# Finishing the message stage's last chunk of nodes in spans of 4, 2 and 1 blocks, with the last block added in the next pass

## The chip, the cores and the metric

The kernel runs on one core of a Trainium2 chip. The metric is the time of one execution in microseconds of device time; the times given are medians of several executions. One further execution was recorded by the hardware profiler, and all profile lines come from it. TensorE is called PE here, VectorE DVE, ScalarE ACT, GpSimd POOL and SyncE SP; PEld are PE's weight loads.

## The reference

A small graph network over N = 6250 nodes with 64 features and E = 206250 directed edges. Every stage normalises each node's row, applies relu, and adds what comes back along the edges. What matters here are the last two stages:

```python
# stage 3: a message for each edge, summed by its end, then a root
x_ = relu(relu(E @ w1 + b1) @ w2 + b2)
msg = sigmoid(x_ @ Bw + Bb) * Vp[src] + (x_ @ Cw + Cb)
M = clip(msg, EPS) ** 2
mean = segment_sum(M, dst) / max(count, 1)
x = x + sqrt(mean)
# stage 4: three rounds of propagation over the same graph
h = maximum(layernorm(x), 0)
embs = acc = h
for _ in range(3):
    embs = segment_sum(norm[:, None] * embs[row], col)
    acc = acc + embs
x = x + acc / 4
```

## The kernel before, in words

**Layout.** The nodes stand in 49 blocks (NB) of 128 rows, seven blocks (CB) to a chunk, seven chunks (NC). The graph is held in DRAM as a dense matrix of edge counts in fp8, `A[c]` for the columns of chunk c. A piece `A[c][:, blocks(k), :]` has 128 x 7 x 896 counts, 784 KB. A sum over neighbours is a matrix product of such pieces with node values; the values are split into three bf16 parts (`split`, L712), which stand in the tile `U3`.

**The message loop** (`slot`, L1599, called from L1645). The edges are sorted by their end and worked on in G = 202 groups of 1024. Slot i does one step of each of several groups: it turns the edge features of group i (L1527), runs the two layers for groups i-1 and i-2 (L1531), the gates and shifts for group i-3 (L1541, L1545), multiplies and clips group i-4 (L1555 to L1557; L1555 reads the rows of `Vp` that POOL has fetched by eight indirect DMAs, L1519, into one of four buffers), squares and splits it, sums group i-5 over its edges (L1578) and adds group i-6 to its nodes in `H` (L1583 ff). PE, DVE and ACT run in the order in which the code is written (`manual_schedule`, L1644).

**What is done beside it.** `todo` is a list of pieces of extra work, and each slot takes n of them (L1616), so many that the list is empty when the next chunk of nodes is finished; half is done ahead of the squares and half at the slot's end. There are three kinds. A *crossing* (L1420) turns up to four 128 x 128 squares of a piece with PE (L1425) and compares them with the mirrored piece by DVE (L1431): the kernel checks that the matrix is symmetric. There are 28 pairs of chunks, each with 14 crossings. A *partial sum* (L1438) multiplies one half (448 columns) of a piece with the values of the seven blocks of chunk i, 21 matmuls of 64 output rows (L750), and DVE adds the result to `Y` (L1450). `here` and `there` load the pieces, through SP's queue. Crossings, partial sums and the squares of the messages share two PSUM buffers, `p_sum`.

**The order of the work.** When the messages of chunk c are complete, `finished(c)` (L1485) divides and takes the root, adds to `X`, normalises and splits the result into `U3`: 14 passes of DVE and four of ACT, one after another. Then `plan` puts the pieces of chunk c into `todo`: the four pairs of `CROSS[c]` and 14 partial sums. So chunks 0 to 5 of the first round's matrix product are summed in the loop. The pairs of `FIRST` fill the slots before chunk 0 is finished. Chunks 0 to 5 are finished at the ends of slots 35, 64, 93, 122, 151 and 180, chunk 6 at the end of slot 207, the last.

**Behind the loop.** For the first round of propagation, only chunk 6's part is left: for every half s, 21 matmuls (L1700 to L1707), the addition to `Y` (L1708), and for every second half seven matmuls with `twice`, which turn `Y` back to nodes (L741), and `propagated` (L1676), which scales and splits the result for the next round. The second and the third round are `gather` (L1180): for every chunk, 49 blocks times seven, one matmul of 192 columns each (L1190), from pieces loaded six ahead.

Of the kernel before, what the change touches and what calls it, by code (L numbers as in the profile page):

```python
# [16 lines left out]
P = 128  # L17
# [600 lines left out]
def fast(ctx, tc, bad, x, src, dst, edge_attr, W3, b3, W4, b4, w1, b1, w2, b2, Bw, Bb, Cw, Cb,  # L618
# [52 lines left out]
    missed = const.tile([P, 3], F32, name="missed")  # L671

    def blocks(c):
        return slice(c * CB, (c + 1) * CB)

    def over_features(v, n=CB):
        return v.unsqueeze(2).to_broadcast([P, n, D])
# [14 lines left out]

    def normed(h, X_c):

        m = stat.tile([P, CB], F32, name="m")
        nc.vector.tensor_reduce(m, X_c, axis=AX.X, op=OP.add)
        nc.vector.tensor_scalar_mul(m, m, 1.0 / D)
        nc.vector.tensor_sub(h, X_c, over_features(m))
        q = stat.tile([P, CB, D], F32, name="q")
        nc.vector.tensor_mul(q, h, h)  # L700
        v = stat.tile([P, CB], F32, name="v")
        nc.vector.tensor_reduce(v, q, axis=AX.X, op=OP.add)
        nc.scalar.activation(v, v, AF.Sqrt, bias=eps, scale=1.0 / D)
        nc.vector.reciprocal(v, v)
        nc.vector.scalar_tensor_tensor(h, h, 0.0, over_features(v), op0=OP.max, op1=OP.mult)

    def of_nodes(pool):

# [1 line left out]

    def split(u, U3, c):
        u3 = U3[:, blocks(c), :, :]  # L712
        nc.scalar.activation(u3[:, :, 0, :], u, AF.Copy)
        r = stat.tile([P, CB, D], F32, name="r")
        nc.vector.tensor_sub(r, u, u3[:, :, 0, :])
        nc.scalar.activation(u3[:, :, 1, :], r, AF.Copy)
        nc.vector.tensor_sub(u3[:, :, 2, :], r, u3[:, :, 1, :])
# [455 lines left out]

    def normed_and_split(h, U3, c, scale):
        normed(h, X[:, blocks(c), :])
        u = stat.tile([P, CB, D], F32, name="u")
        nc.vector.tensor_mul(u, h, over_features(scale[:, blocks(c)]))
        split(u, U3, c)

    def gather(apool, wpool, psum, U3, then, beside=iter(())):  # L1180


        for c in range(NC):
            p = [psum.tile([P, 512], F32, name=f"p_acc{q}") for q in range(4)]
            for k in range(NC):
                t = apool.tile([P, CB, W], COUNT, name="piece")
                nc.sync.dma_start(t, A[c][:, blocks(k), :])
                for d in range(CB):
                    for b in range(CB):
                        nc.tensor.matmul(  # L1190
                            p[d // 2][:, d % 2 * 3 * D:(d % 2 + 1) * 3 * D],
                            t[:, b, d * P:(d + 1) * P],
                            U3[:, k * CB + b, :, :].rearrange("p t f -> p (t f)"),
                            start=(k == 0 and b == 0 and d % 2 == 0),
                            stop=(k == NC - 1 and b == CB - 1 and d in (1, 3, 5, 6)))
                for _ in range(2 - (c > 0 or k > 4)):
                    next(beside, None)
            z = wpool.tile([P, CB, D], F32, name="zg")
            for q in range(4):
                n = min(2, CB - 2 * q)  # L1200
                nc.vector.tensor_reduce(  # L1201
                    z[:, 2 * q:2 * q + n, :],
                    p[q][:, :n * 3 * D].rearrange("p (d t f) -> p d f t", t=3, f=D),
                    axis=AX.X, op=OP.add)
            then(c, z)
# [173 lines left out]
    with ExitStack() as ph:  # L1379
# [9 lines left out]


        CROSS = (((0, 6), (0, 1), (0, 2), (0, 0)), ((1, 6), (1, 2), (1, 3), (1, 1)),
                 ((2, 6), (2, 3), (2, 4), (2, 2)), ((3, 6), (3, 4), (3, 5), (3, 0)),
                 ((4, 6), (4, 5), (4, 0), (4, 1)), ((5, 6), (5, 0), (5, 1), (5, 2)))
        FIRST = ((3, 3), (4, 4), (5, 5), (6, 6))
        unlike = cpool.tile([P, 28 * 2 * CB], F32, name="unlike")

        def order(pairs):
            ks = [k for _, k in pairs]
            return [(pairs[0][0], k)
                    for k in ks + [k for k in range(NC) if (pairs[-1][0], k) not in pairs]]  # L1400

        here_of = list(FIRST) + [at for pairs in CROSS for at in order(pairs)]
        there_of = list(FIRST) + [at for pairs in CROSS for at in pairs]
        held = {}

        def here(n):

            if n < len(here_of):
                i, k = here_of[n]
                t = held["here", i, k] = piece_pool.tile([P, CB, W], COUNT, name="piece")  # L1410
                nc.sync.dma_start(t, A[k][:, blocks(i), :])

        def there(n):

# [23 lines left out]
        def partial(i, s):  # L1438

            t = held["here", i, s // 2]  # L1440
            p = ps_a.tile([P, 512], F32, name="p_sum", bufs=2)
            for b in range(CB):
                spread(p, U3, i * CB + b, t[:, b, s % 2 * CW:(s % 2 + 1) * CW], CW,
                       i * CB, CB)

            def added():
                if i == 0:
# [5 lines left out]

        todo, crossings, asked = [], [], []

        def plan(pairs, sums):
            for at, (i, k) in enumerate(order(pairs) if sums else pairs):
                asked.append((i, k))
                todo.append((here, len(asked)))
                if at < len(pairs):  # L1460
# [21 lines left out]
                if then:  # L1482
                    read.append(then)

        def finished(c):  # L1485

            t = H[:, blocks(c), :]
            nc.vector.tensor_mul(t, t, over_features(n1[:, blocks(c)]))

            nc.vector.tensor_scalar_max(t, t, 1e-30)  # L1490
            nc.scalar.activation(t, t, AF.Sqrt)
            nc.vector.tensor_mul(t, t, over_features(some[:, blocks(c)]))
            nc.vector.tensor_add(X[:, blocks(c), :], X[:, blocks(c), :], t)
            normed_and_split(H[:, blocks(c), :], U3, c, norm3)
            if c < NC - 1:
                plan(CROSS[c], True)

        here(0)
        there(0)
        plan(FIRST, False)  # L1500
        last = {b: g for g in range(G) for b, _, _ in halves(g)}
        ends = [last[c * CB + CB - 1] for c in range(NC)]

        BC_AT, M_AT, SUM_AT, ADD_AT = 3, 4, 5, 6
        of = [{} for _ in range(G)]
        ends = [e + ADD_AT for e in ends]

        def loaded(g):
            of[g]["e"] = mpool.tile([P, J * D], F32, name="e", bufs=6)
# [70 lines left out]
        def added_to_nodes(g):  # L1583
# [5 lines left out]
            for k, (b, q0, q1) in enumerate(halves(g)):  # L1589
# [4 lines left out]
                else:  # L1594
                    nc.vector.tensor_scalar(H[:, b, :], r, part, None, op0=OP.mult)
                    begun.add(b)
            return [b // CB for b, _, _ in halves(g) if last[b] == g and b % CB == CB - 1]

        def slot(i):  # L1599
            def at(later):  # L1600
# [12 lines left out]
            read_them()  # L1613
            if at(1):
                layer(i - 1, w1_d, "eT", "p_1")
            n = -(-len(todo) // max(min(k for k in ends if k >= i) + 1 - i, 1))  # L1616
            some_of(n - n // 2)
            if at(M_AT):
                squared(i - M_AT)
# [16 lines left out]
            some_of(n // 2)  # L1636
            if at(SUM_AT):
                summed(i - SUM_AT)
            for c in done:
                finished(c)  # L1640

        for g in range(4):
            loaded(g)
# [2 lines left out]
                slot(i)  # L1646
            read_them()

        assert not todo and len(crossings) == 28 * 2 * CB


        nc.vector.tensor_reduce(missed[:, 2:3], unlike, axis=AX.X, op=OP.add)
# [14 lines left out]
    with ExitStack() as ph:  # L1667
# [2 lines left out]
        psum = ph.enter_context(tc.tile_pool(name="ps4", bufs=1, space=PSUM, reuse_waits="tile"))  # L1670
        upool = ph.enter_context(tc.tile_pool(name="upool", bufs=1, reuse_waits="tile"))

        for layer in range(3):
            V3 = of_nodes((upool, node)[layer]) if layer < 2 else None

            def propagated(c, y):  # L1676
                z = wpool.tile([P, CB, D], F32, name="z")
                s3 = over_features(norm3[:, blocks(c)])
                nc.vector.tensor_mul(z, y, s3)
                if V3 is not None:  # L1680
                    u = wpool.tile([P, CB, D], F32, name="u")
                    nc.vector.tensor_mul(u, z, s3)
                    split(u, V3, c)
                h = H[:, blocks(c), :]
                nc.vector.tensor_add(h, h, z)
                if V3 is None:
                    o = X[:, blocks(c), :]
                    nc.vector.scalar_tensor_tensor(o, h, 0.25, o, op0=OP.mult, op1=OP.add)
                    lo, hi = c * W, min((c + 1) * W, N)
                    full = (hi - lo) // P  # L1690
                    nc.sync.dma_start(
                        out[lo:lo + full * P, :].rearrange("(b p) f -> p b f", p=P),
                        o[:, :full, :])
                    if lo + full * P < hi:
                        nc.sync.dma_start(out[lo + full * P:hi, :], o[:hi - lo - full * P, full, :])

            if layer:
                gather(apool, wpool, psum, U3, propagated)
            else:
                for s in range(CS):  # L1700
                    if s % 2 == 0:
                        whole = apool.tile([P, CB, W], COUNT, name="piece")
                        nc.sync.dma_start(whole, A[s // 2][:, blocks(NC - 1), :])
                    t = whole[:, :, s % 2 * CW:(s % 2 + 1) * CW]
                    p = psum.tile([P, 512], F32, name="p_sum", bufs=2)
                    for b in range(CB):
                        spread(p, U3, NB - CB + b, t[:, b, :], CW, NB - CB, CB)  # L1707
                    nc.vector.tensor_add(Y[:, s, :], Y[:, s, :], p[:, :CW])  # L1708
                    if s % 2:
                        propagated(s // 2, to_nodes(  # L1710
                            psum, Y[:, s - 1:s + 1, :].rearrange("p s w -> p (s w)"), CB))
            U3 = V3


def gnn_kernel(tc, *args):
# [38 lines left out]
```

## Time and profile before

| what | us |
|---|---|
| median of 3 runs (4157.1 to 4163.57) | 4158.35 |
| the profiled execution | 4192.68 |
| its span, first to last instruction | 4190.8 |
| message loop, first gather of rows to the last slot | about 1000 to 3730 |
| last chunk's finishing (DVE L1488 to L717, then one addition) | 3730.1 to 3740.3 |
| the rest of the first round | 3740 to 3785 |
| second round, first matmul at | 3785.2 |
| third round, to the end | 3983 to 4190.8 |

How the views read: the page gives busy shares in 40 slices of the span (here 104.8 us each), the granted clock of PE in tenths, and the groups of instructions by line. A timeline line has the start in us, the busy time in us, the engine, the source line, the operation, output<-inputs with the shape, the count, and in brackets the idle time of the engine just before and what ended it. A line of a table of stretches has the stretch, its length, the busy time of PE, PEld, DVE, ACT and POOL with the count of instructions, the granted clock of PE, the DMA share and GB/s. In the loop a slot can be told by the start of its L1555: slot i is the (i-3)rd of the 202.

### The profile page before, as it was taken

To read this page: it belongs to the slowest core of one execution; us is meant where nothing else is said; L and a number is where in the kernel's file an instruction comes from. 1 tells how busy PE (TensorE), PEld (TensorE's weight loads), DVE (VectorE), ACT (ScalarE), POOL (GpSimd) and SP (SyncE) were. 2 spreads that over 40 slices of the span, in tenths; PEclk is the share of its full clock that TensorE was granted. 3 is DMA by queue.
4 is the path that set the end of the run, shared out by engine and by line. 5 is a ranking of instruction groups with operands and counts; after the bars stand their busy time and mean duration, and the time that the engine had idled before them with its cause. 6 is when DMAs were issued, how large, how long until landed. Compare 5 with 4: busy or idle time off the path is not lost.

```text
span 4190.8 us, 60773 instructions
## 1 busy us (share of the span) xinstructions
PE 3129.4 (75%) x24366; PEld 2232.6 (53%) x24366; DVE 2074.5 (50%) x5097; ACT 1237.4 (30%) x2061; POOL 1609.1 (38%) x1894
## 2 busy tenths in 40 slices
PE   1799989996665666666676757766766777689999
PEld 1788889994333333333333333433333343349999
DVE  6999934322554544444545544544454454462111
ACT  3677710001333322332333323323332333220000
POOL 5000010002666655655555555556555655510000
PEclk9999999997777778877877777778777787789999
DMA  3243366653222222222222222222222222125665
GB/s 114 56 109 98 97 218 193 197 184 96 58 60 60 58 55 67 57 61 59 64 63 61 59 56 71 60 53 57 75 56 54 63 73 61 45 90 186 200 207 156
DMA packets 229379, 388.81 MB, mean 93 GB/s; under 512 B 93801, under 2 KB 139801, under 8 KB 228830
## 3 DMA queue, kind: packets, MB, share of 16 engines
q1 hardware_dynamic: 170478, 322.28, 24.7%
q0 software_dynamic: 55104, 60.65, 7.2%
q8 instruction: 193, 3.16, 0.3%
q10 hardware_dynamic: 3504, 1.90, 0.2%
q14 instruction: 100, 0.82, 0.1%
HBM read 340.48 MB, written 44.21 MB: 92 GB/s over the span
## 4 chain that ended last, share of the span: by engine, by line
PE 47%; DVE 22%; another core or an unknown queue 12%; issue 10%; ACT 7%; DMA 1%; POOL 0%; ACTq 0%; DVEq 0%; SPq 0%; POOLq 0%
PE p_acc L1190 18%; PE p_bc L1545 7%; PE p_sum L750 5%; PE p L1531 5%; DVE to L1570 3%; DVE hd L888 3%; ACT h L1535 2%; PE p_s L1578 2%; DVE lo L888 2%; DVE m L1555 2%; DVE m L1556 2%; DVE junk L1431 2%; PE p_bc L1541 2%; PE p_sum L1425 2%
## 5 line engine op out<-in xcount | busy, mean ns | idle before, releaser
L1519 POOL DMA_INDIRECT v<-Vp_dram,src_g x1616 | 1537.6, 952 | 1489.9 <-DVE m L1555 682.2
L1190 PE MATMUL p_acc<-U,piece 128*128 128x192 bf16 x9604 | 800.3, 246 | 11.9 <-DMA piece<-A 9.4
L1190 PEld LDWEIGHTS <-piece 128*128 128x128 fp8e4 x9604 | 795.4, 98 | 17.1 <-DMA piece<-A 9.6
L1545 PE MATMUL p_bc<-BC,h 128*128 128x256 f32 x1616 | 582.8, 489 | 33.7 <-issue 32.0
L1425 PE MATMUL p_sum<-ident_b,piece 128*128 128x128 bf16 x1372 | 167.4, 247 | 527.5 <-issue 190.9
L1425 PEld LDWEIGHTS <-piece 128*128 128x128 fp8e4 x1372 | 116.0, 111 | 693.2 <-issue 469.9
L1431 DVE SCALAR_TENSOR_TENSOR junk<-p_sum,there 128x512 bf16<-128x512 f32 (+1 forms) x392 | 242.4, 618 | 489.1 <-remote 329.9
L1545 PEld LDWEIGHTS p_bc<-BC,h 128*128 128x128 f32 x1616 | 339.4, 232 | 206.7 <-issue 170.7
L1555 DVE TENSOR_TENSOR m<-p_bc,v 128x512 f32<-128x512 f32 x202 | 139.7, 691 | 558.9 <-ACT p_bc L1550 444.5
L750 PE MATMUL p_sum<-piece,U 128*64 128x448 fp8e4 x2058 | 287.1, 391 | 109.2 <-issue 91.4
L1535 ACT ACTIVATE h<-p,b_c 128x512 f32<-128x512 f32 x404 | 263.5, 692 | 275.8 <-PE p_sum L1425 116.3
L1531 PE MATMUL p<-h,w_d 128*128 128x512 f32 x404 | 269.6, 748 | 87.7 <-ACT h L1535 58.8
L907 ACT ACTIVATE strip<-p_a 128x784 fp8e4<-128x784 f32 x392 | 301.1, 821 | 100.0 <-PE p_a L903 86.8
L1201 DVE TENSOR_REDUCE zg<-p_acc 128x128 f32<-128x384 f32 x112 | 56.3, 507 | 511.8 <-PE p_acc L1190 511.3
L1570 DVE TENSOR_SCALAR to<-count,lane 128x128 bf16<-128x128 bf16 x1616 | 287.7, 270 | 0.0
L1565 ACT ACTIVATE p_sum<-m 128x512 f32<-128x512 f32 x202 | 120.5, 597 | 528.8 <-DVE junk L1431 251.9
L750 PEld LDWEIGHTS <-U 128*64 128x64 bf16 x2058 | 130.7, 118 | 262.0 <-issue 193.7
L1541 PE MATMUL p_bc<-BC_b,ones 3*128 3x512 bf16 x404 | 183.0, 453 | 116.0 <-DVE m L1556 103.0
L1531 PE MATMUL p<-eT,w_d 128*128 128x512 f32 x404 | 243.7, 684 | 13.3 <-issue 10.1
L1564 ACT ACTIVATE m<-m 128x512 bf16<-128x512 f32 x202 | 127.1, 629 | 404.9 <-DVE m L1557 322.4
L1541 PEld LDWEIGHTS <-ones 3*128 3x128 bf16 x404 | 37.5, 93 | 386.0 <-issue 207.2
L1042 PE MATMUL p_sum<-U,strip 128*128 128x192 bf16 x2401 | 229.4, 247 | 0.0
(212 smaller groups left out, 3573.3 us busy)
## 6 DMA issues: line engine op xcount, KB each, us to landing
piece<-A SPq DMA_DIRECT2D x249, 784.0 KB
e<-in_edge_attr SPq DMA_DIRECT2D x202, 256.0 KB
v<-Vp_dram,src_g POOLq DMA_INDIRECT x1616
A<-strip SPq DMA_DIRECT2D x7, 3136.0 KB
there<-A SPq DMA_DIRECT2D x28, 784.0 KB
A<-strip SPq DMA_DIRECT2D x7, 2352.0 KB
pairs<-pair SPq DMA_DIRECT2D x1, 1616.0 KB
Vp_dram<-v SPq DMA_DIRECT2D x7, 224.0 KB
```

The source lines that it names most:

```text
L750: nc.tensor.matmul(p[half * D:(half + 1) * D, :w], U3[:, b, k, :], at_block, start=(i < 2), stop=(i >= 3 * n - 2))
L907: nc.scalar.activation(strips[s][:, :, col:col + 2 * SG].rearrange("p b (j l) -> p b j l", l=2), p[:, :, :2 * NB].rearrange("p j (b l) -> ...
L1042: nc.tensor.matmul(p[:, d * 3 * D:(d + 1) * 3 * D], strips[s][:, b, (d0 - lo + d) * P:(d0 - lo + d + 1) * P], U3[:, b, :, :].rearrange("p ...
L1190: nc.tensor.matmul(p[d // 2][:, d % 2 * 3 * D:(d % 2 + 1) * 3 * D], t[:, b, d * P:(d + 1) * P], U3[:, k * CB + b, :, :].rearrange("p t f - ...
L1425: nc.tensor.matmul(p[:, a - a0, :], held["here", i, k][:, a, b * P:(b + 1) * P], ident_b, start=True, stop=True)
L1431: nc.vector.scalar_tensor_tensor(junk[:, :(a1 - a0) * P], p[:, :a1 - a0, :].rearrange("p a q -> p (a q)"), 15.5, of_there, op0=OP.min, op1 ...
L1519: nc.gpsimd.indirect_dma_start(out=v[:, j, :], out_offset=None, in_=Vp_dram[:, :], in_offset=bass.IndirectOffsetOnAxis(ap=src_g[:, g, j:j ...
L1531: nc.tensor.matmul(of[g][p], w, of[g].pop(x), start=True, stop=True)
L1535: nc.scalar.activation(of[g][t], of[g].pop(p), **how)
L1541: nc.tensor.matmul(p_bc[:, 4 * b:4 * b + 4].rearrange("p j o f -> p (j o f)"), ones, BC_b, start=True, stop=False)
L1545: nc.tensor.matmul(p_bc[:, 2 * q:2 * q + 2].rearrange("p j o f -> p (j o f)"), h2[:, q * P:(q + 1) * P], BC, start=False, stop=(k == 1))
L1570: nc.vector.tensor_scalar(to[:, j, :], count, lane[:, g, j:j + 1], None, op0=OP.is_equal)
```

## The change

The last chunk is no longer finished in one piece. Its blocks 42 to 45 are finished when their messages are complete (slot 196), blocks 46 and 47 at slot 205, and block 48 at slot 207. `finished` takes a first block and a number, and the helpers below it work on that many blocks.

- The partial sums of the span of four (14 times 12 matmuls) are planned two slots later and spread over slots 198 to 205; those of the span of two (14 times 6 matmuls) all stand in slot 207. `here` loads only the rows of the span.
- Block 48 isn't added by a partial sum. Its seven rows of pieces are loaded into one tile, `held["rest"]`, and `with_the_rest` adds it in PSUM: for each block of a chunk, the turn of `Y` by `twice` is left open, and three matmuls with the piece as weights and `U3` of block 48 as data are accumulated onto it. Then follows `propagated`.
- `with_the_rest` runs inside the second round's first chunk: `gather` takes one step of `ahead` for each piece, the first step doing chunks 0 and 1. This gather's PE and DVE instructions stand in the order of the code.
- As chunk 5's partial sums must now be done by slot 196, two of its four pairs move: (5,6) to `FIRST`, and (2,5) to chunk 2's window, slots 94 to 122. Chunk 5 keeps two.
- In the loop a chunk's work is planned at the start of the slot after its finishing; in `propagated` the addition to `H` is written ahead of the split.

The core of the diff:

```diff
-                 ((2, 6), (2, 3), (2, 4), (2, 2)), ((3, 6), (3, 4), (3, 5), (3, 0)),
-                 ((4, 6), (4, 5), (4, 0), (4, 1)), ((5, 6), (5, 0), (5, 1), (5, 2)))
-        FIRST = ((3, 3), (4, 4), (5, 5), (6, 6))
+                 ((2, 6), (2, 3), (2, 4), (2, 2), (2, 5)), ((3, 6), (3, 4), (3, 5), (3, 0)),
+                 ((4, 6), (4, 5), (4, 0), (4, 1)), ((5, 0), (5, 1)))
+        FIRST = ((3, 3), (4, 4), (5, 5), (6, 6), (5, 6))
+        SPANS = [(c * CB, CB) for c in range(NC - 1)] + [(NB - CB, 4), (NB - 3, 2), (NB - 1, 1)]
...
+                if here_of[n] is None:
+                    held["rest"] = t
+                    for k in range(NC):
+                        nc.sync.dma_start(t[:, k, :], A[k][:, NB - 1, :])
+                    return
...
-            for b in range(CB):
-                spread(p, U3, i * CB + b, t[:, b, s % 2 * CW:(s % 2 + 1) * CW], CW,
-                       i * CB, CB)
+            b0, rows = (i * CB, CB) if i < NC else (i, dict(SPANS)[i])
+            for b in range(rows):
+                spread(p, U3, b0 + b, t[:, b, s % 2 * CW:(s % 2 + 1) * CW], CW, b0, rows)
...
-        def finished(c):
+        def finished(b0, n):
...
-        ends = [e + ADD_AT for e in ends]
+        ends = [e + ADD_AT for e in ends[:-1]] + [G + ADD_AT - 3]
+        planned = {}
...
-            n = -(-len(todo) // max(min(k for k in ends if k >= i) + 1 - i, 1))
+            for args in planned.pop(i, ()):
+                plan(*args)
+            n = -(-len(todo) // max(min([k for k in ends if k >= i] or [i]) + 1 - i, 1))
...
-            for c in done:
-                finished(c)
+            for b0, n in done:
+                finished(b0, n)
+                if n == CB:
+                    planned[i + 1] = [(b0 // CB, CROSS[b0 // CB], True)]
+                elif b0 < NB - 1:
+                    planned[i + 2] = [(b0, (), True)]
...
+        def with_the_rest(V3):
+
+            y = Y.rearrange("p s w -> p (s w)")
+            for c in range(NC):
+                p = psum.tile([P, 512], F32, name="p_node", bufs=2).rearrange("p (b f) -> p b f", f=D)
+                for k in range(CB):
+                    d = slice((c * CB + k) * P, (c * CB + k + 1) * P)
+                    nc.tensor.matmul(p[:, k, :], y[:, d], twice, start=True, stop=False)
+                    for t in range(3):
+                        nc.tensor.matmul(p[:, k, :], held["rest"][:, c, k * P:(k + 1) * P],
+                                         U3[:, NB - 1, t, :], start=False, stop=(t == 2))
+                propagated(V3, c, p[:, :CB, :])
+                if c:
+                    yield
...
+        with tc.manual_schedule(engines={ET.PE, ET.DVE}):
+            gather(apool, wpool, psum, U1, second, ahead=with_the_rest(U1))
+        gather(apool, wpool, psum, U2[0], lambda *args: propagated(None, *args))
```

## The prediction

> **What bounds the kernel now.** I read the page's slices first, then the groups by line, then the timelines of VectorE (DVE) and TensorE (PE), because the change touches two places: the message loop (about 1045 to 3730 us) and the joint behind it (3730 to 3785).
>
> ```profile
> PE   1799989996665666666676757766766777689999
> ...
> PEclk9999999997777778877877777778777787789999
> ...
> L1519 POOL DMA_INDIRECT v<-Vp_dram,src_g x1616 | 1537.6, 952 | 1489.9 <-DVE m L1555 682.2
> ```
>
> In the loop (slices 11 to 35) no engine is full and the granted clock is 0.7 to 0.8: each slot is a round trip. GpSimd fetches a group's rows (eight gathers, about 10.1 us) and then waits until VectorE has read an older buffer at L1555. The starts of L1555 therefore measure the slots, and they run in pairs:
>
> ```profile
> 1288.61 0.69 DVE L1555 TENSOR_TENSOR m<-p_bc,v 128x512 f32<-128x512 f32 x1 [7.01 <-ACT p_bc L1550]
> ...
> 1312.74 0.69 DVE L1555 TENSOR_TENSOR m<-p_bc,v 128x512 f32<-128x512 f32 x1 [11.34 <-ACT p_bc L1550]
> ...
> 1768.81 0.69 DVE L1555 TENSOR_TENSOR m<-p_bc,v 128x512 f32<-128x512 f32 x1 [2.37 <-ACT p_bc L1550]
> ...
> 1798.00 0.69 DVE L1555 TENSOR_TENSOR m<-p_bc,v 128x512 f32<-128x512 f32 x1 [1.42 <-ACT p_bc L1550]
> ...
> 1834.77 0.69 DVE L1555 TENSOR_TENSOR m<-p_bc,v 128x512 f32<-128x512 f32 x1 [1.84 <-ACT p_bc L1550]
> ```
>
> With one or two crossings a slot a pair takes 24.1 us (12.1 a slot). With three partial sums in a pair it takes 29.2, and with a chunk's finishing in it 36.8. Three crossings a slot, sustained, take 56.7 us in slots 106 to 109 (14.2 a slot), but 49.8 in slots 100 to 103 (12.5), after a long slot that let GpSimd catch up. So work is free up to two crossings a slot and costs beyond that.
>
> Behind the loop everything hangs on one chain, then on PE:
>
> ```profile
> 3730.09 0.62 DVE L1488 TENSOR_TENSOR H<-H,n 128x448 f32<-128x448 f32 x1
> ...
> 3739.68 0.62 DVE L717 TENSOR_TENSOR U<-r,U 128x448 bf16<-128x448 f32 x1 [0.64 <-ACT U L716]
> ```
> ```profile
> 3727.25 4.35 PE L750 MATMUL p_sum<-piece,U 128*64 128x448 fp8e4 x42
> 3738.44 0.58 PE L750 MATMUL p_sum<-piece,U 128*64 128x448 fp8e4 x1 [6.84 <-ACT U L713]
> 3739.70 7.36 PE L750 MATMUL p_sum<-piece,U 128*64 128x448 fp8e4 x41 [0.68 <-ACT U L716]
> ...
> 3748.30 1.10 PE L741 MATMUL p_node<-twice,Y 128*128 128x64 f32 x8
> ...
> 3785.19 0.58 PE L1190 MATMUL p_acc<-U,piece 128*128 128x192 bf16 x5
> ```
>
> Finishing the last chunk takes 10.2 us (3730.1 to 3740.3). Then the remaining pass, 14 halves of 21 matmuls and seven turns to nodes, fills PE until the first gather at 3785.2. That is 45 us.
>
> **The change, part by part** (in the profiled execution's time).
>
> *First window, slots 0 to 35.* The pair (5,6) adds 14 crossings, so that all slots hold two, where slots 24 to 35 had one. Two a slot: 242.5 us in slots 4 to 23, 12.12 each. One a slot: 120.2 in slots 24 to 33, 12.02 each. 12 x 0.1 = **+1** (0 to +3). It also adds one 784 KB load on SP's queue, ahead of the edge loads there; DMA is 22 to 24% busy, so I cost it at nothing; uncovered it would be about 2 us (seven such loads passed in 14 us, 3726 to 3740).
>
> *Chunk 2's window, slots 94 to 122 (399.5 us now).* The pair (2,5) moves here: 14 more crossings, each some 4 matmuls and a VectorE pass (0.69 + 0.08). Slots 111 to 116, light now (73.7 us), become three-crossing slots like 73 to 78 (85.6): +12. Slots 95 to 97 get a fourth piece: about +1. The tail 117 to 122 (93.8) becomes three such slots (42.6), one at 13.0 like slot 52, two of two partials (about 15 each, from 29.2 a pair with three), and the finishing (5): 90.6, so -3. Together **+10**; bounds +3 (the 12.5 us rate) and +16 (14.2 throughout, and 2 us more for each fourth).
>
> *Slots 181 to 201 (279.3 us now).* Chunk 5 loses 28 crossings, and its 14 partials must be done by slot 196 instead of 207. Slots 181 to 190 hold the same plus one: +1. Slots 191 to 196 (87.8) now hold twelve partials of 21 matmuls: 13 + 5 x 15 = 88, and the new finishing of four blocks. A finishing in the loop made a pair 36.8 instead of 29.2 (+7.6), at chunk 4's end 32.5 (+3.3); with it go two ACT table loads (1.28 each, at L1491 and L1550). For four blocks I take 4.5, so +5. Slots 197 to 201 (62.3) have an empty slot and four with two partials of 12 matmuls (1.3 us each at 0.107): 12.1 + 4 x 12.3 = 61, so -1. Together **+5**. Lower bound -4: the pair after a long slot runs at 12 again. Upper +15: the 21 matmuls fall in half clock, 3.8 us instead of 2.25 (41 took 7.36 at 3739.7), in half of the twelve, and the 12s cost as the 21s do.
>
> *From slot 202 to the gather (3694.1 to 3785.2, 91.1 us now).* Slots 202 to 204 (24.1) lose two full partials net, where PE was full: 21.7. L1555 to the finishing's start: 5.7. The finishing of n blocks: eleven DVE passes of 448 columns (0.62; 7 columns take 0.17, so 1.02 ns a column) and three ACT passes (0.58 against 0.30) shrink; 10.2 becomes 7.6 for four, 5.9 for two, 5.0 for one. Two blocks: 5.9, exposed, because the span's partials wait for it. Then 14 partials of 6 matmuls, all in slot 207: PE 0.64 each, VectorE's addition 0.62 with two PSUM buffers, 0.73 each; at half clock 1.1 to 1.3; I take 0.9 and 0.7 for the last messages between them: 13.3. Queued behind these on VectorE stands the last block's finishing: 5.0. Then the first chunk's rest: per block two fp32 passes (1.10/8) and three of the rest piece. The nearest row for these is L1425 (fp8 weights, 0.057 apart), the far one L1190 (0.082): 7 x (0.28 + 0.17) = 3.2, at most 3.7. VectorE and ACT follow with 3.9, beside chunk 1's rest. With some half clock (PE idles during both finishings) 9.7 to the first gather matmul. Sum 21.7 + 5.7 + 5.9 + 13.3 + 5.0 + 9.7 = 61.3. The gather is PE work without gaps (198.2 busy of 198.2 in 3785.2 to 3983.4), so the five other rests are added to it: 5 x 3.2 = 16. 91.1 - 77.3 = **-14**; bounds -20 (all at full clock) and -7 (all of it at half).
>
> The DMAs: SP's queue now holds seven loads of 458 KB, seven of 229 KB and seven of 115 KB instead of seven whole pieces at 3723.9, with gather pieces between them. The pieces that the gather needs first are issued before the last small loads, and the gather's 199 GB/s is met by a queue that moved 424 GB/s at 3731.6 to 3735.3. Nothing, at worst 3 us, inside the bounds above. A chunk's VectorE and ACT work (3.9) lies under one piece and one rest (4.04 + 3.2). POOL's queue is unchanged.
>
> Sum: +1 + 10 + 5 - 14 = **+2 us** on 4192.68 (span 4190.8). The median of the unprofiled runs is 4158.35, 0.992 of it; +2 stays +2: **4160**.
>
> The clock, where a rule speaks against the change:
>
> ```profile
> 3735.30:3745.50 10.20, 6.30 (x30) 2.76 (x32) 4.44 (x8) 1.45 (x3) 0.00 (x0) 0.50 0.17 70
> 3745.50:3785.20 39.70, 39.70 (x357) 25.56 (x354) 25.71 (x43) 6.92 (x12) 0.00 (x0) 1.00 0.37 123
> ```
>
> PE was idle 6.8 us from 3731.6, and the granted clock was 0.50 for 10.2 us from 3735.3. The Trainium skill, "TensorE: Matmul & The Clock Gate", Part 1 (the HAM clock gate), says that one idle window of about 3.4 us halves the clock until a busy one. By that rule both new idle stretches (5.9 and 5.0) would be punished in full, by an estimate of some 4 us beyond what I took, and the sum would be +6 instead of +2.
>
> **Rivals.**
> 1. *The loop absorbs the moved work.* For it: 49.8 us for slots 100 to 103, and five slots after each finishing at 11.6. Against it: 14.2 in slots 106 to 109. Then the window of chunk 2 costs +3 and slots 181 to 201 -1: 0 + 3 - 1 - 14 = -12, **4146**.
> 2. *Slower: partials at half clock in the crowded slots.* Twelve partials in slots 191 to 196 stand in PE's order ahead of the gates (L1545) that L1555 waits for. At half clock each costs 1.6 more, about half of that new: +10 there, and the joint brings only -10: 1 + 10 + 15 - 10 = +16, **4174**. It decides if the granted clock in these slots falls under about 0.7 (0.77 now in 3500 to 3700).
> 3. *The rest is not hidden in the gather:* each chunk's piece waits for VectorE as the first does, 5 x 3.9 = +20: **4180**. Against it: the rest of chunk c+1 is issued before piece c.
>
> **How the numbers follow.** Within 0.2% (8.3 us, about what a measurement of this kernel can tell from no change): 0.40, the forecast. Rival 1: 0.27, faster. Rivals 2 and 3: 0.29 and 0.04, slower. The loop's costs and the joint's gain nearly cancel, each known to some 7 us; the range takes in both sides: 4143 to 4180.
>
> **What would show it.** Slots 94 to 122 at about 410 us (403 or less speaks for rival 1); slots 181 to 201 at 284; from slot 202 to the gather's first matmul 61; the first gather 16 longer than 198; 14 partials in about 13 us. I am wrong if GpSimd's waits in slots 111 to 122 stay as they are, or if the granted clock in the joint is 1.0 throughout.

## The result and the profile after

The changed kernel took 4169.86 us (median of 20 runs, 4146.09 to 4190.52), the kernel before 4154.66 (20 runs, 4128.76 to 4170.47): ratio **1.0048**, interval 1.0029 to 1.0067. Two more measurements of the same pair gave 0.9993 (0.9971 to 1.0014) and 0.9955 (0.9942 to 0.9969). In the last set of runs, from which 0.9955 comes, every kernel ran at a level some 660 us lower (the kernel before at 3496.57); for the first three sets the level was 4155 to 4158. The first two intervals don't meet, so that at the upper level the medians do not settle the sign; by the stages below there is almost no change. Ratios are of the fast runs alone; one run of before_free, at 10379.99 us, is among those left out.

The page of the changed kernel:

```profile
PE   1799989996676666666676666766766775879999
...
PEclk9999999997778777777887887778787787889999
...
PE 45%; DVE 23%; another core or an unknown queue 13%; issue 10%; ACT 6%; DMA 1%; POOL 0%; DVEq 0%; ACTq 0%; SPq 0%; POOLq 0%
...
L1531 POOL DMA_INDIRECT v<-Vp_dram,src_g x1616 | 1537.5, 951 | 1502.1 <-DVE m L1567 704.3
```

The loop looks as before: GpSimd idles 1502 us, 704 of them until VectorE has read a buffer (now L1567). The third line is the chain of waits: 13% of the span is put down to a releaser that the trace doesn't know. The joint, in the timelines of VectorE and TensorE:

```profile
3730.11 0.29 DVE L1501 TENSOR_TENSOR H<-H,n 128x128 f32<-128x128 f32 x1
...
3735.37 0.29 DVE L718 TENSOR_TENSOR U<-r,U 128x128 bf16<-128x128 f32 x1 [0.38 <-ACT U L717]
...
3750.63 0.22 DVE L1501 TENSOR_TENSOR H<-H,n 128x64 f32<-128x64 f32 x1
...
3755.01 0.22 DVE L718 TENSOR_TENSOR U<-r,U 128x64 bf16<-128x64 f32 x1 [0.32 <-ACT U L717]
```
```profile
3738.31 6.87 PE L751 MATMUL p_sum<-piece,U 128*64 128x448 fp8e4 x48
3746.35 4.27 PE L751 MATMUL p_sum<-piece,U 128*64 128x448 fp8e4 x36 [1.18 <-DMA piece<-A]
...
3763.64 4.81 PE L1193 MATMUL p_acc<-U,piece 128*128 128x192 bf16 x49
...
3770.59 4.21 PE L1193 MATMUL p_acc<-U,piece 128*128 128x192 bf16 x49
```

Finishing two blocks takes 5.5 us (3730.11 to 3735.66), the 14 partial sums fill the time to 3750.6, finishing one block takes 4.6, and the second round starts at 3763.64 instead of 3785.19. Between the gather's first two pieces stands the rest of chunk 2 (3768.3 to 3770.6).

The stages, measured between starts of L1555 (after: L1567) and the gathers' first matmuls, in two records of each kernel (the second of each comes from the runs below):

| stage, us | before | after | predicted | measured (means) |
|---|---|---|---|---|
| first gather of rows to the end of slot 35 | 433.5, 432.2 | 439.1, 439.5 | +1 | +6.5 |
| chunk 2's window, slots 94 to 122 | 399.5, 395.5 | 397.9, 392.1 | +10 | -2.5 |
| slots 181 to 201 | 279.2, 275.4 | 291.1, 289.4 | +5 | +13.0 |
| slot 202 to the second round | 91.1, 88.4 | 60.4, 60.1 | -29.8 | -29.5 |
| second and third round | 405.6, 405.7 | 418.7, 418.8 | +16 | +13.1 |
| **sum** | | | **+2** | **+0.6** |
| the four windows whose plan is the same | 1581.2, 1545.6 | 1572.1, 1548.1 | 0 | -3.3 |

The last row is why single records mislead: four windows with the same instructions differ by 36 us between two records of one kernel. The whole spans, 4190.8 and 4182.4, would have said -8. The sum is no surer than some 5 us either: chunk 2's window alone differs by 6 us between the two records after.

### The profile page after: what moved, and what is told of

Read it like the earlier page. It is cut to its first block, busy times and chain, and to the rows that moved or that the text cites. A ratio compares the mean times of both kernels' runs of the same rounds, so it can differ in the third digit from the quotient of the medians.

```text
span 4182.4 us, 61063 instructions
## 1 busy us (share of the span) xinstructions
PE 3121.3 (75%) x24471; PEld 2231.3 (53%) x24471; DVE 2085.3 (50%) x5139; ACT 1241.3 (30%) x2071; POOL 1608.8 (38%) x1894
## 4 chain that ended last, share of the span: by engine, by line
PE 45%; DVE 23%; another core or an unknown queue 13%; issue 10%; ACT 6%; DMA 1%; POOL 0%; DVEq 0%; ACTq 0%; SPq 0%; POOLq 0%
PE p_acc L1193 18%; PE p_bc L1557 6%; PE p L1543 5%; PE p_sum L751 4%; DVE to L1582 4%; DVE hd L889 2%; DVE lo L889 2%; PE p_s L1590 2%; DVE junk L1443 2%; DVE m L1567 2%; ACT h L1547 2%; PE p_sum L1437 2%; DVE m L1568 2%; PE p_bc L1553 2%
## 5 line engine op out<-in xcount | busy, mean ns | idle before, releaser
L1557 PE MATMUL p_bc<-BC,h 128*128 128x256 f32 x1616 | 566.0, 478 | 30.5 <-issue 29.7
L1443 DVE SCALAR_TENSOR_TENSOR junk<-p_sum,there 128x512 bf16<-128x512 f32 (+1 forms) x392 | 242.6, 619 | 504.2 <-remote 380.2
L1557 PEld LDWEIGHTS p_bc<-BC,h 128*128 128x128 f32 x1616 | 329.0, 226 | 194.5 <-issue 161.0
L1567 DVE TENSOR_TENSOR m<-p_bc,v 128x512 f32<-128x512 f32 x202 | 139.7, 692 | 509.5 <-ACT p_bc L1562 409.6
```

The costliest lines, as they stand in the source:

```text
L1443: nc.vector.scalar_tensor_tensor(junk[:, :(a1 - a0) * P], p[:, :a1 - a0, :].rearrange("p a q -> p (a q)"), 15.5, of_there, op0=OP.min, op1 ...
L1557: nc.tensor.matmul(p_bc[:, 2 * q:2 * q + 2].rearrange("p j o f -> p (j o f)"), h2[:, q * P:(q + 1) * P], BC, start=False, stop=(k == 1))
```

## The experiments

Theory at the start: the loop's costs and the joint's gain cancel as the prediction had them (P), against a rival in which the moved pairs cost nothing and the crowded slots before 197 cost more (T).

### First set: the parts alone

**moves_only**, the kernel before with the new order of the pairs:

```diff
-                 ((2, 6), (2, 3), (2, 4), (2, 2)), ...
+                 ((2, 6), (2, 3), (2, 4), (2, 2), (2, 5)), ...
-                 ... ((5, 6), (5, 0), (5, 1), (5, 2)))
-        FIRST = ((3, 3), (4, 4), (5, 5), (6, 6))
+                 ... ((5, 0), (5, 1)))
+        FIRST = ((3, 3), (4, 4), (5, 5), (6, 6), (5, 6))
```

> The kernel before with only the pairs moved ((5,6) to the first window, (2,5) to chunk 2's window); the last chunk is finished in one piece as before. Theory P (the moved pairs cost what the prediction said, +1 and +10): slots 94 to 122 take 10 us more than a window with the same plan as before; slots 181 to 207 hold 42 pieces instead of 70 and lose about 16 us (15 fewer third crossings at 1.4, less the partial sums' shift); in all -5 us, ratio 0.999. Theory T (the moved pairs cost nothing, the change's loss arises in slots 181 to 196 from the crowded partial sums and the finishing of four blocks): slots 94 to 122 as in the other windows (390 to 400), slots 181 to 207 -16, in all -15 us, ratio 0.9965.

Measured: ratio 1.0011 (0.9981 to 1.0041); the interval takes in theory P's 0.999 and not T's 0.9965. The stages speak for T: chunk 2's window took 389.3 us, no longer than the others (380.0 to 397.3). Slots 181 to 204 took 285.0 instead of 303.4 and 297.5 (-15, near what both said for slots 181 to 207). But the first window took 441.4, 8 to 9 more than before, which neither had.

**no_pairs**, the changed kernel without the two pairs:

```diff
-                 ((2, 6), (2, 3), (2, 4), (2, 2), (2, 5)), ...
-        FIRST = ((3, 3), (4, 4), (5, 5), (6, 6), (5, 6))
+                 ((2, 6), (2, 3), (2, 4), (2, 2)), ...
+        FIRST = ((3, 3), (4, 4), (5, 5), (6, 6))
+        nc.vector.memset(unlike, 0.0)
```

> The changed kernel without the two moved pairs: the 28 crossings of (5,6) and (2,5) are left out, so that the symmetry of these two pairs of chunks isn't compared; all sums are complete. Theory P: 11 us under the changed kernel, that is +5 to +9 us on the kernel before (ratio 1.0015 to 1.002). Theory T: the same as the changed kernel within 3 us, +15 to +20 us on the kernel before (ratio 1.004 to 1.005).

Measured: ratio 1.0010 (0.9980 to 1.0040), below what either said, and the interval reaches both. The stages are plainer: chunk 2's window 394.9 with 56 crossings, 397.9 and 392.1 with 70, so (2,5) cost nothing over the whole window; the first window 431.6, so (5,6) in `FIRST` costs some 8 us; slots 181 to 201 295.3, no shorter than in the changed kernel, so the pairs have no part in that.

**span6**, the last chunk in spans of 6 and 1:

```diff
-        SPANS = ... + [(NB - CB, 4), (NB - 3, 2), (NB - 1, 1)]
+        SPANS = ... + [(NB - CB, 6), (NB - 1, 1)]
```

> The changed kernel with the last chunk in spans of 6 and 1 blocks instead of 4, 2 and 1. Chunk 5's partial sums are then due by slot 205 again, there is no finishing of four blocks in slot 196, and slot 207 holds 14 partial sums of 18 matmuls. Behind slot 205 it is longer than the changed kernel by 18 us (finishing of six 9.2 instead of 5.5, 14 times 12 matmuls more at 0.085 to 0.107). Theory P (slots 181 to 204 of the changed kernel cost only +5): they become 10 us shorter here; in all +8 us on the changed kernel, ratio to the kernel before about 1.006. Theory T (these slots cost the change 20 us and more): they become 30 us shorter, in all 12 us under the changed kernel, ratio 1.002.

Measured: ratio 1.0016 (0.9983 to 1.0049), as T expected, though the interval takes in much. Slots 181 to 204 took 283.9, 26 to 28 less than in the changed kernel; slot 205 to the second round 55.0 instead of 39.2 (+16, expected +18). So the early deadline of chunk 5's sums, the finishing of four blocks and the partial sums that follow it cost 26 to 28 us together, where P had 10.

**before_again**:

> The kernel before once more, for a second record of its stages. Theory T: the windows of chunks 1 to 4 (388.7 to 400.7 in the first record) are shorter here on the whole, since the first record was taken at 4192.68 and the median is 4155; theory P needs the windows of the first record to hold within 3 us each.

Measured: 4143.06 us, 50 less than the first record; two of the windows of equal plan were 17 us shorter. P's condition (within 3 us) failed: a window's length in one record isn't a price.

With seven records, chunk 2's window can be taken apart:

| slots, us | without (2,5): before, before_again, no_pairs | with it: after, after_again, moves_only, span6 | predicted | measured (means) |
|---|---|---|---|---|
| 94 to 97 | 49.5, 50.1, 48.2 | 53.5, 53.0, 53.6, 53.4 | +1 | +4 |
| 98 to 110 | 182.3, 179.7, 181.5 | 165.7, 161.1, 159.3, 165.1 | 0 | -18 |
| 111 to 116 | 73.8, 72.5, 72.3 | 84.7, 79.4, 81.9, 81.8 | +12 | +9 |
| 117 to 122 | 93.9, 93.2, 92.8 | 94.0, 98.7, 94.6, 93.4 | -3 | +2 |

The price that the prediction put on slots 111 to 116 came. But slots 98 to 110 gave it back: they hold nearly as many pieces as before (VectorE reads 36 instead of 37), on other slots. Why that order is cheaper isn't shown.

### Where the loop loses

Slot by slot, the changed kernel's first window loses 5.8 us in slot 35: it takes 18.1 us in both records of before and in no_pairs, 23.9, 24.0 and 23.2 in after, after_again and span6. (Only in moves_only is it 18.3; there the short and long slots changed places in slots 5 to 8, at 6.8 us, and slot 35 came behind a long one.) VectorE's timeline in slot 35, before and then after:

```profile
1421.41 0.55 DVE L1431 SCALAR_TENSOR_TENSOR junk<-p_sum,there 128x384 bf16<-128x384 f32 x1
...
1421.88 0.62 DVE L1488 TENSOR_TENSOR H<-H,n 128x448 f32<-128x448 f32 x1
```
```profile
1423.18 0.68 DVE L1649 TENSOR_TENSOR m<-p_sum,m 128x512 bf16<-128x512 f32 x1
1429.42 0.69 DVE L1443 SCALAR_TENSOR_TENSOR junk<-p_sum,there 128x512 bf16<-128x512 f32 x1 [5.56 <-remote]
...
1430.04 0.62 DVE L1501 TENSOR_TENSOR H<-H,n 128x448 f32<-128x448 f32 x1
```

In both kernels the reading of a crossing (L1431, L1443) stands in VectorE's order just ahead of chunk 0's finishing. Before, it did not wait. With the pair, slots 24 to 35 have a second crossing, and VectorE sat idle for 5.6 us ahead of the reading, though TensorE had done the four matmuls that it reads by 1421.13 (the ends of matmuls are modelled in the profile):

```profile
1420.74 0.39 PE L1437 MATMUL p_sum<-ident_b,piece 128*128 128x128 bf16 x4
```

The finishing's 10 us begin that much late. Why the signal is late in this kernel and not in the one before isn't shown. Slot 196 is the same on a larger scale: TensorE, VectorE and GpSimd in the changed kernel:

```profile
3614.05 2.27 PE L751 MATMUL p_sum<-piece,U 128*64 128x448 fp8e4 x21
...
3620.64 0.35 PE L751 MATMUL p_sum<-piece,U 128*64 128x448 fp8e4 x1 [0.32 <-issue]
3622.04 0.53 PE L751 MATMUL p_sum<-piece,U 128*64 128x448 fp8e4 x1 [1.05 <-issue]
3622.75 0.53 PE L751 MATMUL p_sum<-piece,U 128*64 128x448 fp8e4 x1 [0.18 <-issue]
```
```profile
3630.49 0.62 DVE L1462 TENSOR_TENSOR Y<-Y,p_sum 128x448 f32<-128x448 f32 x1 [13.00 <-remote]
```
```profile
3645.67 1.03 POOL L1531 DMA_INDIRECT v<-Vp_dram,src_g  x1 [18.04 <-DVE m L1567]
```

The 21 matmuls of one partial sum, which just before took 2.27 us, trickle from 3618.3 to 3631.8 with nothing recorded that they wait for. VectorE's 13.0 us of waiting are not for these but for the sum ahead of them: its matmuls were done at 3616.3, and VectorE could read it at 3630.49. It adds the trickling sum at 3634.30, the finishing of four starts behind that (3634.83), and GpSimd, which had filled all four buffers by 3627.6, waits 18.0. Slots 193 to 196 take 76.0 and 71.6 us, against 56.0 and 55.0 before; but before they hold crossings there and no partial sums, and slots 191 and 192 take 10 to 11 us less after. Over slots 191 to 196 it is 96.3 and 93.2 against 87.8 and 86.4. In both places GpSimd was in the second of two batches of eight gathers without a pause (1422.0 to 1431.9; 3618.0 to 3627.6).

The traces show more of it. In slots 36 to 205 of the ten records at the upper level, the starts of neighbouring matmuls of a partial sum lie on average 0.10 to 0.11 us apart in the first 10 us of a batch of gathers, 0.35 to 0.44 in the rest of the batch, and 0.21 to 0.25 while GpSimd pauses. So TensorE is slow at certain times of GpSimd's rhythm; what makes it slow isn't shown by that.

### Second set: finishing without an extra piece ahead of it

New theory (W): the finishing stands behind the reading of an extra piece whose signal comes late. Rival (R): only the two-slot rhythm shifts. Three kernels empty `todo` one slot earlier, so that no slot that ends with a finishing has an extra piece (for the kernel before, likewise):

```diff
-            n = -(-len(todo) // max(min([k for k in ends if k >= i] or [i]) + 1 - i, 1))
+            n = -(-len(todo) // max(min([k for k in ends if k >= i] or [i]) - i, 1))
```

> The changed kernel once more, against the kernel before. By the sums of the stages of the records so far (first window +7.5, chunk 2's window -3, slots 181 to 201 +16, the joint and the gathers -17) it should be +3 us, ratio 1.0008; by the first measurement of the medians +20 us, ratio 1.0048 (1.0029 to 1.0067). The stages should repeat: slot 35 23 to 24 us, slots 193 to 196 76 us, slot 205 to the first gather 39 us.

> The changed kernel with no extra piece in a slot that ends with a finishing of the loop: the list is emptied one slot earlier. Theory W (the finishing stands on VectorE behind the reading of an extra piece whose signal from TensorE comes late while GpSimd issues its gathers, so it falls behind the gathers instead of beside them): slot 35 takes 18 us instead of 23.5, slots 64, 93, 122, 151 and 180 18 to 21 instead of 26 to 30, slot 196 20 instead of 29; the slots ahead take 2 to 4 us more for the displaced pieces. In all about -25 us on the changed kernel, ratio to the kernel before 0.996 to 0.999. Theory R (only the two-slot rhythm shifts, the finishing costs the same wherever the pieces stand): the windows of the chunks stay at 390 to 398 and slots 191 to 196 at 96, ratio as the changed kernel's, 1.003 to 1.005.

> Spans of 6 and 1 blocks, and no extra piece in a slot that ends with a finishing. Against the run with spans of 6 and 1 (ratio 1.0016): theory W -20 us (slot 35 -5.5, five finishings of chunks -8 each, +4 each for the displaced pieces), ratio 0.997; theory R: the same, 1.0016.

> The kernel before with no extra piece in a slot that ends with a finishing. Slot 35 has one crossing there now and takes 18.1, and should lose at most 1. Theory W: slots 64, 93, 122 and 151 take 18 to 21 instead of 26 to 30; in all -15 us, ratio 0.9965. Theory R: the same within 5 us, ratio 0.999 to 1.001.

| kernel | ratio to before | slot 35 | slots 64, 93, 122, 151, 180 | slot 196 |
|---|---|---|---|---|
| after_again | 0.9993 (0.9971 to 1.0014) | 24.0 | 25.6, 26.5, 31.7, 19.3, 28.4 | 27.1 |
| after_free | 0.9964 (0.9938 to 0.9990) | 18.3 | 30.5, 29.8, 19.1, 18.6, 29.0 | 16.9 |
| span6_free | 0.9954 (0.9921 to 0.9986) | 18.3 | 30.0, 19.6, 18.4, 19.1, 19.3 | no finishing |
| before_free | 0.9954 (0.9928 to 0.9980) | 18.1 | 19.4, 30.0, 30.5, 19.8, 29.4 | no finishing |

Slot 35 and slot 196 fall as W says. The other finishings do not: with and without an extra piece they take either 18 to 21 or 26 to 32 us. In all 50 of them in the ten records the long value stands behind a slot of at most 10.8 us and the short one behind a slot of at least 11.5, so it is the rhythm (R) there. Slots 191 to 196 keep 92.4 of 93.2 to 96.3 us although slot 196 itself lost 10: the displaced partial sums cost it elsewhere. All three freed kernels are 0.4 to 0.5% faster than the kernel before, with intervals that exclude 1: near the ratios that W gave, but not from the slots that W named. Where the gain lies isn't settled: slots 36 to 180 together take 1923 to 1952 us in their records and 1940 to 1981 in the seven records without the freeing, which overlap. The split of the last chunk adds nothing to it that can be seen: 0.9964 with, 0.9954 without.

### Third set: the cover

What covers the moved crossings? If it is GpSimd's gathers, they must cost something once these are halved. In the two half kernels `fetched` fetches four of the eight rows, and L1567 reads each twice:

```diff
-            v = of[g]["v"] = mpool.tile([P, J, D], F32, name="v", bufs=4)
-            for j in range(J):
+            v = of[g]["v"] = mpool.tile([P, J // 2, D], F32, name="v", bufs=4)
+            for j in range(J // 2):
```

> The changed kernel a third time, since two measurements gave 1.0048 (1.0029 to 1.0067) and 0.9993 (0.9971 to 1.0014). If the sum of the stages is right (+1 us from the records of both), 0.999 to 1.002; if the first measurement is right, 1.003 or more.

> The kernel before with the two pairs moved as in the change, the last chunk finished in one piece, and no extra piece in a slot that ends with a finishing. Theory L (the moved pairs are absorbed in chunk 2's window, and slots 181 to 204 gain by losing 28 crossings): the first window +2, chunk 2's window 0, slots 181 to 204 285 instead of 300, so -13 us on the kernel before with the same freeing (0.9954): ratio 0.992. Theory M (what is taken from the late slots comes back in the earlier ones): the same as that kernel, 0.995 to 0.996.

> The changed kernel with only four of the eight gathers of each group; the other half of the rows is taken from the same four, so that the messages are not the reference's. GpSimd's work of a slot is 5 us instead of 10.1. If GpSimd's gathers are what covers the moved crossings, the slots with two crossings fall well under 12.1 (to 8 or 9), and chunk 2's window (70 crossings) is 8 to 15 us longer than in the same kernel without the two pairs. If the crossings have room on TensorE and VectorE whatever GpSimd does, the two windows are equal within 3 us.

> The same as the run before it (four of eight gathers), and without the 28 crossings of (5,6) and (2,5), so that these two pairs aren't compared either. Chunk 2's window holds 56 crossings: 8 to 15 us shorter than in the run before it if the gathers are the cover, equal within 3 us if not; the first window (56 crossings instead of 70) likewise.

All four ran at the lower level. **after_third** 3480.38 us, ratio 0.9955 (0.9942 to 0.9969), faster, against its expectation from the stages (0.999 to 1.002). **moves_free** (moves_only and the freeing together) 3494.57, ratio 0.9996 (0.9987 to 1.0005): neither L (0.992) nor M (0.995 to 0.996). What differs is seen in the longest waits, of after_again (4147.8 us) and then after_third (3477.1); columns are total us, times, longest:

```profile
POOL v L1531 <- DVE m L1567: 662.5, 110, 19.6
...
DVE junk L1443 <- remote: 313.5, 52, 19.1
```
```profile
DVE m L1567 <- DMA v<-Vp_dram,src_g: 491.9, 145, 6.4
...
POOL v L1531 <- issue: 455.0, 1493, 0.3
```

At the lower level GpSimd issues gather after gather with nothing but its own 0.30 us between (a slot is 10.05 us), VectorE waits for the rows, and none of its waits is put down to "remote" any more. The matmuls of partial sums start 0.10 to 0.11 us apart in slots 36 to 205 of after_third and moves_free, though GpSimd's gathers never pause there. The chain of waits of after_third:

```profile
PE 31%; POOL 28%; DVE 17%; issue 13%; DMA 8%; ACT 4%; ACTq 0%; DVEq 0%; POOLq 0%; SPq 0%
```

There the loop absorbs the moved work. The ratio of moves_free, 0.9996, shows no cost of the moved pairs in sum; for the rest, moves_free stands in for the kernel before, of which there is no record at this level: slots 181 to 204 233.5 and 232.7, from slot 205 to the second round 39.2 and 65.7 (-26.5), the two rounds 419.4 and 405.5 (+13.9). Finishing slots are 16.0 to 18.6 everywhere.

With half the gathers (3137.57 and 3128.25 us, one run each) chunk 2's window is 250.3 us with (2,5) and 244.0 without, and slots 4 to 35 take 238.1 with (5,6) and 233.7 without. So 14 crossings cost 6.3 and 4.4 us of their own, 0.3 to 0.45 each, between the two expectations (8 to 15, or within 3); slots 4 to 34, with two crossings each, take 7.1 us instead of the 8 or 9 expected. With all gathers, at the same level, chunk 2's window is 293.8 and 291.3, on average 3.4 and 0.0 us above the four windows of equal plan in its own record. So at the lower level, where GpSimd sets the pace, its gathers cover a part of the crossings' cost or all of it. At the upper level, where GpSimd idles 1502 us, no run tests this.

## Why the prediction was right, and where it was wrong

The forecast, no change (+2 us), agrees with the sum of the stages (+0.6) at the level at which it was made; the first measured ratio, 1.0048, lies above it, inside the range, and the second, 0.9993, on it. By the prediction's own band for no change, 0.2%, the first and the third measurement are changes, one each way. And the sum of the stages comes out only because its steps failed in opposite directions, which is luck: two came some 6 and 8 us dearer than forecast, one some 12 us cheaper.

- **First window, +1: measured +6.5**, and +7.5 over all seven records. The price per slot was right (slots 4 to 34 took 367.8 us with the pair, 369.9 without). What I left out was the step from one crossing to two in the slot that ends with a finishing. In after_free, without a piece there, slot 35 takes 18.3 us instead of 23.9, and the window with the pair 434.8 (435.3 in span6_free) against 432.0 in before_free: +3, the upper bound that I gave. moves_only is the exception: it lost as much, but in slots 5 to 8.
- **Chunk 2's window, +10: measured -2.5.** The price of slots 111 to 116 was nearly right, +9 of +12 in the seven records. What failed is the term for the slots ahead: it had the extra piece of slots 95 to 97 (+1) and nothing for slots 98 to 110, and these took 18 us less. The rule behind it, that work is free up to two crossings a slot and costs beyond that, has no place for such a gain. Rival 1 (+3) is nearer in size here, but not in mechanism: where the third crossings stand in slots 111 to 116, they cost.
- **Slots 181 to 201, +5: measured +13.** Slots 181 to 190 came to +7.3 instead of +1, slots 191 to 196 to +7.6 instead of +5, and slots 197 to 201 to -1.9 instead of -1. Some of it lies in where the long slots fall: slot 190 is a long one after (20.0 and 18.8 us instead of 14.5 and 15.3). In slot 196 it is the late signals. This is the place of rival 2, not its mechanism: the granted clock was 0.78 in 3568.7 to 3644.7, against 0.80 in the same four slots before, and not under the 0.7 that it needs.
- **From slot 202 to the second round, 61.3: measured 60.4 and 60.1.** Term by term, in the first record: 21.7 was 21.2; 5.7 was 5.6; finishing two 5.9 was 5.5; partial sums 13.3 was 15.0; finishing one 5.0 was 4.6; to the first gather matmul 9.7 was 8.4.
- **The rests, 16: measured 13.1.** In the second round it is 11.5, five rests of 2.3 us (3768.29 to 3770.59) instead of 3.2. The other 1.6 are a longer third round, which no run explains. TensorE has no gap in the second round, so VectorE's part lay beside the gather and rival 3 fell.
- **The DMAs, nothing:** one wait of 1.18 us for a piece among the partial sums.

The clock, in TensorE's timeline and in the table of stretches of the changed kernel:

```profile
3729.72 1.48 PE L751 MATMUL p_sum<-piece,U 128*64 128x448 fp8e4 x12 [4.15 <-DVE m L1649]
...
3754.48 0.19 PE L1723 MATMUL p_node<-U,piece 128*128 128x64 bf16 x1 [3.49 <-ACT U L714]
```
```profile
3731.00:3738.30 7.30, 2.96 (x18) 2.08 (x16) 4.33 (x15) 0.92 (x4) 0.00 (x0) 0.50 0.43 143
3738.30:3751.00 12.70, 11.22 (x87) 5.95 (x87) 8.59 (x17) 0.00 (x0) 0.00 (x0) 0.89 0.69 232
...
3755.00:3763.60 8.60, 8.52 (x67) 8.42 (x67) 3.79 (x7) 1.15 (x2) 0.00 (x0) 0.50 0.53 195
```

Twice the granted clock fell to 0.50 behind an idle TensorE: after 4.15 us that end at 3729.72, which is ahead of the finishing of two and not in it as predicted, and after 3.49 us in the finishing of one. The Trainium skill, "TensorE: Matmul & The Clock Gate", Part 1 (the HAM clock gate), has it that an idle window of about 3.4 us does so. But the 4 us that I had estimated from it on top did not come: the joint took 60.4, not 65.

The signs that the prediction named came out mixed: slots 94 to 122 took 397.9 and 392.1, where 403 or less was to speak for rival 1; slots 181 to 201 took 291.1 and 289.4 instead of 284. Neither sign of being wrong came: GpSimd's idle time in slots 111 to 122 rose from 62.9 and 60.7 us to 67.9 and 65.8, and the clock in the joint was not 1.0 throughout.

At the lower level rival 1 was right as a whole: the loop absorbs the moved work, and the joint's gain is left, -16 us (0.0045 of 3496.57), or -12.6 by the stages above, against its -12.

What stays open: why two measurements at the same level give 1.0048 and 0.9993, when the stages that differ sum to +0.6; where the freed kernels' 0.4% lies; and why TensorE is slow at the upper level.

## What to carry to other kernels

Gain at the joint behind a loop can be read off a timeline almost to the microsecond; the price of work moved into a loop cannot be read from one record, if slots of equal content vary by more than the price: compare windows of equal plan first. Extra work is nearly free under an engine that paces the loop without a pause, as GpSimd does at the lower level. At the upper level extra pieces just ahead of a long serial chain cost 6 us in slot 35 and 10 in slot 196 (of which the slots ahead took most back when they were moved there), and nothing that can be seen at the five other finishings. And measure again where the kernel runs at another pace: the same change was within measurement at one level and -0.45% at the other.

## What the runs showed of the hardware

- **TensorE runs slowly and its signals come late at certain times of GpSimd's gathers, at the upper level only.** Behind the first 10 us of a batch, neighbouring matmuls of a partial sum start 0.35 to 0.44 us apart instead of 0.10 to 0.11. GpSimd's own rate is the same at both levels (0.95 us a gather and 0.30 between). In the chains of waits 10 to 13% of the span is put down to an unknown releaser in all ten records at the upper level, and nothing in the four at the lower. Gathers without a pause are not enough to cause it: in after_third and moves_free, at the lower level, GpSimd never pauses in slots 36 to 205, and the distance is 0.10 to 0.11 us throughout. Whether they are needed for it is open; no run took them away at the upper level.
- **The level:** the same kernel took 4157 and 3497 us in different sets of runs, with a spread of 60 us at the upper and 5 us at the lower. The loop makes almost all of it: from the first gather of rows to the second round before_again took 2737.1 us and moves_free 2095.6, up to the first gather 998.3 and 990.1, in the last two rounds 405.7 and 405.5. What sets the level isn't known. The three sets of experiments ran on three chips, 5, 8 and, at the lower level, 11, so that it may go with the chip; no chip was seen at both levels, and for the first measurement the chip isn't on record.
